# Three adds per block of a two-layer model: from VectorE to accumulating DMAs of GpSimd, in blocks 1 to 7

## The chip, the cores and the metric

The kernel runs on one core of a Trainium2 chip. A core has TensorE (PE, matrix products into PSUM), VectorE (DVE, elementwise work and scans), ScalarE (ACT, activations), GpSimd (POOL) and SyncE (SP, which only issues DMAs), and 16 DMA engines that move data between HBM and the on-chip memory SBUF. Every engine works off its own list of instructions in order, and semaphores tie the lists together. The metric is the device time of one execution in microseconds (us). An accumulating DMA is a transfer that adds what it brings to what already stands at its destination.

## What is computed

A float32 input x of 4 sequences of 1024 tokens with 256 features runs through two layers. What matters here is layer 0:

```python
x = L0_attn_x
xn = _layernorm(x)
# attention branch, with Fourier features of the queries and keys
x2 = _layer_norm(xn, ln1_g, ln1_b)
attn = linear_attention(x2 @ wq + bq, x2 @ wk + bk, x2 @ wv + bv)
s = xn + (attn @ wo + bo)                        # bo: attention's output bias
s = s + (relu(_layer_norm(s, ln2_g, ln2_b) @ w1 + b1) @ w2 + b2)   # b2: the MLP's second bias
# gate branch: token shift, squared relu, sigmoid
g = _silu(token_shift_ffn(xn))
x = x + s * g
```

Layer 1 takes the layer norm of this x, runs a state-space scan over the tokens (512 channels with 16 states each) on one branch and a mixture of 8 experts, top 2, on the other, and gives `x + s * silu(moe)`.

## The kernel before

**Blocks.** The 4096 tokens are cut into eight blocks j = 0 to 7 of 512 tokens (`NBLK`, `TB`), two for each sequence. A block's tile by tokens is `[128, 4, 256]`: 128 partitions, four tokens on each, 512 KB in all.

**Streams.** The program is written as several generators (`before_attention`, `after_attention`, `experts`, and the scans of layer 1 with what prepares them) that a loop advances in turns, so that layer 0 of later blocks stands between the scan steps of earlier ones. The scans are 256 steps of a block's half with one state each (`scan_step`: L1113 multiplies, L1116 and L1122 scan, L1131 multiplies by the output weights, L1134 sums over the states on TensorE).

**Order.** `arrange` plans the order of the instructions of TensorE, VectorE and ScalarE from estimated durations and buffers: forward and backward passes of list scheduling, with hand-set offsets in the table `LATER`. GpSimd's and SyncE's lists are placed by the framework. In the planner a DMA of GpSimd costs its issue, its bytes at 260 per ns and a fixed landing time; it has no separate price for a DMA that accumulates.

**The path of one block through `after_attention`.** x1 is the block's residual tile, in one of four work buffers.

- L540 (`fetch_x`) loads the input rows into x1 with a GpSimd DMA, and L614 (`apply`) normalizes them on VectorE.
- L622 transposes x1 on TensorE (tiles `tr_xnb`); L690 copies the result to `xnt` on ScalarE, for the gate branch.
- L704 adds the output projection (PSUM tile `po`) to x1 in two halves. L705 adds the bias bo.
- L598 to L614 (`normalize`, `apply`) make x3 from x1: bn_stats and their aggregation on VectorE, a power on GpSimd (L601), a subtraction and multiplication on VectorE. L711 then adds the bias b2 to x1.
- The MLP runs in two halves. Its output (PSUM tile `py`) is added to x1 at L748, four times in all.
- The gate branch makes g. A second load of the input rows (L540, tile xi) is issued, L791 multiplies x1 by g, L793 adds xi.
- L794 stores x1 as x_mid with a GpSimd DMA. L598 to L614 normalize x1 into xi (`st_cb`, `rs_cb`), L797 stores xi, TensorE transposes it (`tr_gb`), and L802 stores the transposed tile, which `prepare_block` of layer 1 loads (L956).

`prepare_block` convolves over four groups of channels (L975 on VectorE, with a memset of GpSimd at L965 ahead of each group in the first block of a sequence). The biases lie in SBUF as `bias_s`, copied to all partitions once at the start. The lines after the change are 12 to 18 higher: L704 becomes L717, L748 becomes L760, L791 becomes L806, L794 becomes L812.

Of the kernel before, what the change touches and what calls it, by code (L numbers as in the profile page):

```python
# [15 lines left out]
F32 = mybir.dt.float32  # L16
U32 = mybir.dt.uint32
AF = mybir.ActivationFunctionType
ALU = mybir.AluOpType
# [4 lines left out]
P = 128  # L24
NB, L, D = 4, 1024, 256
TB = 512
NBLK = NB * L // TB
NT = TB // P
# [448 lines left out]
def kernel(  # L477
# [3 lines left out]
    nc = tc.nc  # L481
# [19 lines left out]
    def col(name, i=0):  # L501
        return vec[:, COL[name] + i : COL[name] + i + 1]

    def tokens(ap):
        return ap.rearrange("(t p) d -> p t d", p=P)
# [30 lines left out]
    work = l0.enter_context(tc.tile_pool(name="work0", bufs=4))  # L536

    def fetch_x(j):
        t = work.tile([P, NT, D], F32, name=f"x_{j}_{nc.next_id()}", tag="w")
        nc.gpsimd.dma_start(out=t, in_=tokens(x[j * TB : (j + 1) * TB, :]))  # L540
        return t
# [8 lines left out]
        out=bias_s, in_=rows_a.rearrange("a d -> (a d)").partition_broadcast(P)  # L550
# [61 lines left out]
    def apply(dst, src, mv, rs):  # L612
        for t in range(NT):
            nc.vector.tensor_scalar(  # L614
                dst[:, t, :], src[:, t, :], mv[:, t, 0:1], rs[:, t : t + 1], ALU.subtract, ALU.mult
            )
# [13 lines left out]
    def bias(n, tiles=NT):  # L630

        return bias_s[:, n : n + 1, :].to_broadcast([P, tiles, D])

    def before_attention(b, s):
# [36 lines left out]
            nc.vector.tensor_tensor(v[:, 2 * i : 2 * i + 2, :D], ps, bias(0, 2), ALU.add)  # L671
        keys[b, s] = (qt, kt, v)

    last_col = {}

    def after_attention(b, s, at):

        j = b * (L // TB) + s
        tag = f"b{j}"
        x1 = fetch_x(j)  # L680
# [10 lines left out]
        if s == 0:  # L691
            last_col[b] = small.tile([P, NC, 1], F32, name=f"last_{tag}", tag="last")
            nc.gpsimd.tensor_copy(last_col[b], xnt[:, :, TB : TB + 1])
        yield "N"
        for i in range(NT // 2):
            ps = bank(f"po_{tag}{i}").rearrange("p (u d) -> p u d", u=2)
# [5 lines left out]
                )  # L702
            x12 = x1[:, 2 * i : 2 * i + 2, :]
            nc.vector.tensor_tensor(x12, ps, x12, ALU.add)  # L704
        nc.vector.tensor_tensor(x1, x1, bias(1), ALU.add)  # L705
        waiting[0] -= NC
        yield "N"
        mv, rs = normalize(small, x1, tag)
        x3 = work.tile([P, NT, D], F32, name=f"x3_{tag}", tag="w")
        apply(x3, x1, mv, rs)  # L710
        nc.vector.tensor_tensor(x1, x1, bias(2), ALU.add)  # L711
        yield "N"
        x3t = work.tile([P, NC, TB], F32, name=f"x3t_{tag}", tag="w")
        for c in range(NC):
            nc.scalar.activation(
                x3t[:, c, :], transposed(x3, c, f"{tag}{c}"), AF.Identity,
                bias=col("ln2_b", c), scale=col("ln2_g", c),  # L717
# [69 lines left out]
            yield "S"  # L787
        special(g, g, AF.Silu, scale=0.5)
        yield "N"
        xi = fetch_x(j)  # L790
        nc.vector.tensor_tensor(x1, x1, g, ALU.mult)  # L791
        yield "N"
        nc.vector.tensor_tensor(x1, x1, xi, ALU.add)  # L793
        nc.gpsimd.dma_start(out=tokens(x_mid[j]), in_=x1)  # L794
        mv, rs = normalize(small, x1, f"c{tag}")
        apply(xi, x1, mv, rs)
# [903 lines left out]
    for b in range(NB):  # L1700
        groups = [("k", b, s, t) for s in range(2) for t in range(NT)]
        groups += [("q", b, s, m, par) for s in range(2) for m in range(NC) for par in range(2)]
        for c, group in enumerate(groups):
            if c == 0:
                before.add(before_attention(b, 1))
            elif c == (4 if b else 3):
                while before.force():
                    pass
            elif c == 12 and b + 1 < NB:
                before.add(before_attention(b + 1, 0))  # L1710
            if before.wants == "K" and c >= 12:
                before.wants = "N"
            following = groups[c + 1] if b == 0 and c + 1 < len(groups) else None
            if b == 0 and c in (8, 12):
                empty_slots(c // 4 - 2, features(begun[group], 0)[:, 0, :])
            cycle(
                group, quota=(2, 3 if scans.ahead else 6, 2 if scans.ahead else 6, 0),
                following=following,
            )
            for s in range(2):  # L1720
                if len(at.get((b, s), ())) == NC:
                    after.add(after_attention(b, s, at.pop((b, s))))
            if 0 in ready and not blocks and not scans.side.todo:
                scans.side.add(first_unit())
                while not units:
                    scans.side.force()
        while before.force():
            pass
# [87 lines left out]
```

## Time and profile before

| | us |
|---|---|
| median of 3 runs | 2163.91 (2161.5 to 2171.76) |
| the profiled execution, its own time | 2169.19 |
| its span | 2167.5 |
| VectorE busy | 1923.6 |
| TensorE busy | 1732.6 |
| ScalarE busy | 1396.3 |
| GpSimd busy | 484.7 |

The span runs from the first to the last instruction. A group of instructions is one line with one engine, operation and tile; it is shown with its count, its busy time, the mean duration of one in ns, and the idle time of the engine just ahead of it with what ended that idle time. A line such as "DVE x L614 <- POOL rs_cb L601: 1.9, 2, 0.9" in the list of waits says that VectorE waited 1.9 us in total, 2 times, at most 0.9 us, for GpSimd's instruction at L601. In the timeline a line begins with its start and its duration. For a GpSimd DMA the duration is that of its issue, not of the transfer. The clock that the throttle granted to TensorE was 0.88 of full speed on average.

By time, layer 0 of block 0 ends at about 210 us, the first scan begins at 279.8 us, layer 0 of block 7 ends at about 1281 us; from there on the scans share the core with the experts. The three adds start at these times (us), by block:

| line | 0 | 1 | 2 | 3 | 4 | 5 | 6 | 7 |
|---|---|---|---|---|---|---|---|---|
| L705 (bo) | 136.9 | 240.8 | 467.3 | 628.2 | 782.8 | 937.3 | 1089.9 | 1191.1 |
| L711 (b2) | 144.2 | 251.6 | 474.9 | 659.7 | 810.9 | 947.7 | 1097.6 | 1200.0 |
| L793 (xi) | 208.8 | 360.0 | 582.4 | 732.6 | 890.2 | 1049.1 | 1163.5 | 1271.0 |

### The profile page before, as it was taken

To read this page: it belongs to the slowest core of one execution; us is meant where nothing else is said; L and a number is where in the kernel's file an instruction comes from. 1 tells how busy PE (TensorE), PEld (TensorE's weight loads), DVE (VectorE), ACT (ScalarE), POOL (GpSimd) and SP (SyncE) were. 2 spreads that over 40 slices of the span, in tenths; PEclk is the share of its full clock that TensorE was granted. 3 is DMA by queue.
4 is the path that set the end of the run, shared out by engine and by line. 5 is a ranking of instruction groups with operands and counts; after the bars stand their busy time and mean duration, and the time that the engine had idled before them with its cause. 6 is when DMAs were issued, how large, how long until landed. Compare 5 with 4: busy or idle time off the path is not lost. (4 is left out here: it accounts for less than half of the span.)

```text
span 2167.5 us, 25198 instructions
## 1 busy us (share of the span) xinstructions
PE 1732.6 (80%) x9052; PEld 1193.5 (55%) x9052; DVE 1923.6 (89%) x2511; ACT 1396.3 (64%) x2057; POOL 484.7 (22%) x445
## 2 busy tenths in 40 slices
PE   7888798789988889979798865278897887899764
PEld 3435455445655446645466644266776576667643
DVE  5764499999999899999899999879898998899999
ACT  5862588888896988878866463235454644465594
POOL 1001001011100111100111021844354235453200
PEclk9879798899999999979898987589998999999867
DMA  6352234323433333423345462577777767677553
GB/s 119 114 199 59 70 83 112 111 55 99 111 97 104 107 84 93 125 51 116 98 108 137 115 202 78 152 231 226 243 216 226 239 194 232 221 232 253 172 171 102
DMA packets 139934, 311.88 MB, mean 144 GB/s; under 512 B 21329, under 2 KB 41041, under 8 KB 133921
## 3 DMA queue, kind: packets, MB, share of 16 engines
q1 hardware_dynamic: 107120, 167.24, 29.3%
q0 software_dynamic: 32688, 143.03, 18.8%
q8 instruction: 72, 1.18, 0.2%
q14 instruction: 54, 0.43, 0.1%
HBM read 254.08 MB, written 56.14 MB: 143 GB/s over the span
## 5 line engine op out<-in xcount | busy, mean ns | idle before, releaser
L588 ACT ACTIVATE da<-dt,neg_a 128x512 f32<-128x512 f32 x512 | 338.6, 716 | 163.6 <-PE y L1134 101.7
L1134 PE MATMUL y<-ident,da 128*128 128x128 f32 x2048 | 306.4, 298 | 131.8 <-DVE da L1131 99.8
L1134 PEld LDWEIGHTS y<-ident,da 128*128 128x128 f32 x2048 | 258.5, 154 | 202.8 <-issue 94.9
L1116 DVE TENSOR_TENSOR_SCAN h<-da,h 128x1024 f32<-128x1024 f32 x128 | 291.8, 2282 | 22.7 <-ACT da L588 12.3
L1131 DVE TENSOR_TENSOR da<-h,bcs 128x1024 f32<-128x1024 f32 x256 | 310.4, 1215 | 0.2
L1113 DVE TENSOR_TENSOR h<-dtu,bcs 128x1024 f32<-128x1024 f32 x240 | 289.0, 1210 | 12.9 <-DMA bcs<-bcd 12.7
L1122 DVE TENSOR_TENSOR_SCAN h<-da,h_tail,h 128x512 f32<-128x512 f32 x224 | 278.1, 1269 | 2.4 <-ACT da L588 1.9
L463 ACT ACT_TABLE_LOAD x150 | 192.4, 1283 | 3.4 <-PEq L1801 0.8
L515 PE MATMUL ph<-xst,we 128*128 128x256 f32 (+1 forms) x736 | 159.0, 368 | 20.0 <-ACT xst L1464 20.0
L515 PE MATMUL po<-we,ht 128*128 128x256 f32 x624 | 156.3, 399 | 11.7 <-ACT ht L1477 8.1
L515 PEld LDWEIGHTS ph<-xst,we 128*128 128x128 f32 x736 | 129.0, 201 | 43.4 <-ACT xst L1464 24.8
L515 PEld LDWEIGHTS po<-we,ht 128*128 128x128 f32 x624 | 121.1, 201 | 39.0 <-ACT ht L1477 12.2
L515 PE MATMUL ph_b<-x3t_b,w_b 128*128 128x512 f32 x256 | 122.6, 625 | 8.2 <-DVE fs_k L859 3.7
L1477 ACT ACTIVATE ht<-ph,we 128x256 f32<-128x256 f32 (+1 forms) x184 | 69.3, 438 | 77.6 <-PE ph L515 51.4
L515 PE MATMUL py_b<-w_b,ht_b 128*128 128x256 f32 x512 | 115.8, 382 | 3.4 <-ACT ht_b L737 1.9
L515 PEld LDWEIGHTS py_b<-w_b,ht_b 128*128 128x128 f32 x512 | 96.3, 191 | 22.2 <-issue 4.1
L859 DVE SCALAR_TENSOR_TENSOR fs_k<-fs_k,fk 128x512 f32<-128x512 f32 x128 | 80.7, 677 | 22.0 <-ACT fs_k L858 21.9
L900 PE MATMUL kv<-fs_k,v_a 128*32 128x256 f32 x1024 | 79.6, 447 | 19.3 <-ACT fs_k L588 19.1
L858 ACT ACTIVATE fs_q<-fq,round_c 128x512 f32<-128x512 f32 x112 | 68.3, 684 | 38.7 <-PE fq L834 32.0
L1414 POOL DMA_INDIRECT fused<-xs x39 | 81.9, 2100 | 43.0 <-DVE xs L1497 33.3
L1437 POOL DMA_INDIRECT we<-in_wcat_dram,wrow x46 | 73.3, 1592 | 62.6 <-issue 34.2
L515 PEld LDWEIGHTS ph_b<-x3t_b,w_b 128*128 128x128 f32 x256 | 48.7, 199 | 67.4 <-issue 50.5
(256 smaller groups left out, 3387.2 us busy)
## 6 DMA issues: line engine op xcount, KB each, us to landing
bcs<-bcd SPq DMA_DIRECT2D x240, 512.0 KB, 5.5
x<-in_x_dram POOLq DMA_DIRECT2D x23, 512.0 KB
slots<-blank SPq DMA_DIRECT2D x1, 9984.0 KB
xs<-slots POOLq DMA_DIRECT2D x16, 516.0 KB
w_b<-in_w_dram POOLq DMA_DIRECT2D x16, 512.0 KB
w_b<-in_w_dram POOLq DMA_DIRECT2D x32, 256.0 KB
slots<-blank SPq DMA_DIRECT2D x1, 4992.0 KB
xs<-slots POOLq DMA_DIRECT2D x16, 260.0 KB
```

The source lines that it names most:

```text
L463: order[engine].append(nc.scalar.preload_act_table_set(TABLES[k]).ins)
L515: nc.tensor.matmul(ps, lhs, rhs, start=i == 0, stop=i == len(pairs) - 1)
L588: nc.scalar.activation(out, in_, func, **kw)
L859: nc.vector.scalar_tensor_tensor(t[:, 1, :], t[:, 0, :], -ROUND, ps[r], ALU.add, ALU.subtract)
L900: nc.tensor.matmul(kv[b][r // 2][32 * g : 32 * g + 32, r % 2, :, :], v[:, t, h * DH : (h + 2) * DH], f[:, :, m, par, :], start=(s, t, r % ...
L1113: nc.vector.tensor_tensor(h, dtu, bcs[:, 0:1, :].to_broadcast([P, UNIT, TB]), ALU.mult)
L1116: nc.vector.tensor_tensor_scan(flat, da.rearrange("p w t -> p (w t)"), flat, 0.0, ALU.mult, ALU.add)
L1122: nc.vector.tensor_tensor_scan(h[:, w, :], da[:, w, :], b[w], h_tail[:, c, n : n + 1], ALU.mult, ALU.add,)
L1131: nc.vector.tensor_tensor(da, h, bcs[:, 1:2, :].to_broadcast([P, UNIT, TB]), ALU.mult)
L1134: nc.tensor.matmul(y[:, t, w * P : (w + 1) * P], da[:, w, t * P : (t + 1) * P], ident, is_transpose=True, start=False, stop=(n, t % 2, w) ...
L1414: i = nc.gpsimd.indirect_dma_start(out=dst, out_offset=IndirectOffsetOnAxis(ap=index, axis=0), in_=src, in_offset=None)
L1437: nc.gpsimd.indirect_dma_start(out=w, out_offset=None, in_=wcat, in_offset=IndirectOffsetOnAxis(ap=wrow[:, k, i : i + 1], axis=0),)
```

## The change

In blocks 1 to 7 each of the three adds of VectorE becomes a GpSimd DMA with `accum_op=ALU.add` and x1 as destination. For the two biases the source is the bias row in HBM (`rows_a`, 1 KB), repeated for all partitions and tokens; for the input rows it is the block of x itself, so that the load into xi is gone and xi is a work buffer that `apply` first writes. The bias bo is now added after the transposes of x1 and ahead of the projection's add (it stood behind that add). Block 0 keeps VectorE's adds, with bo moved ahead in the same way.

```diff
+    def add_rows(j, x1, src):
+
+        nc.gpsimd.dma_start(out=x1, in_=src, accum_op=ALU.add)
+
+    def add_bias(j, x1, n):
+
+        if j == 0:
+            nc.vector.tensor_tensor(x1, x1, bias(n), ALU.add)
+        else:
+            row = rows_a[n].partition_broadcast(P)
+            add_rows(j, x1, row.unsqueeze(1).to_broadcast([P, NT, D]))
+
     last_col = {}
...
             nc.gpsimd.tensor_copy(last_col[b], xnt[:, :, TB : TB + 1])
+        add_bias(j, x1, 1)
         yield "N"
...
             nc.vector.tensor_tensor(x12, ps, x12, ALU.add)
-        nc.vector.tensor_tensor(x1, x1, bias(1), ALU.add)
         waiting[0] -= NC
         yield "N"
         mv, rs = normalize(small, x1, tag)
         x3 = work.tile([P, NT, D], F32, name=f"x3_{tag}", tag="w")
         apply(x3, x1, mv, rs)
-        nc.vector.tensor_tensor(x1, x1, bias(2), ALU.add)
+        add_bias(j, x1, 2)
         yield "N"
...
-        xi = fetch_x(j)
+        if j == 0:
+            xi = fetch_x(j)
+        else:
+            xi = work.tile([P, NT, D], F32, name=f"xi_{tag}", tag="w")
         nc.vector.tensor_tensor(x1, x1, g, ALU.mult)
         yield "N"
-        nc.vector.tensor_tensor(x1, x1, xi, ALU.add)
+        if j == 0:
+            nc.vector.tensor_tensor(x1, x1, xi, ALU.add)
+        else:
+            add_rows(j, x1, tokens(x[j * TB : (j + 1) * TB, :]))
         nc.gpsimd.dma_start(out=tokens(x_mid[j]), in_=x1)
```

## The prediction

> **What bounds the kernel now.** I read the busy line and the slices of the page first, then a table by stretch, then VectorE's waits inside the stretch that the edit touches, and last the rows of the three adds and of the nearest transfers.
>
> ```profile
> PE 1732.6 (80%) x9052; PEld 1193.5 (55%) x9052; DVE 1923.6 (89%) x2511; ACT 1396.3 (64%) x2057; POOL 484.7 (22%) x445
> ...
> DVE  5764499999999899999899999879898998899999
> ```
>
> ```profile
> 130.00:285.00 155.00, 124.86 (x528) 72.54 (x521) 79.03 (x153) 75.78 (x114) 18.26 (x26) 0.87 0.26 83
> 285.00:1290.00 1005.00, 854.30 (x4592) 544.84 (x4591) 961.37 (x1265) 782.73 (x1036) 116.42 (x154) 0.91 0.38 107
> 1290.00:2167.00 877.00, 650.74 (x3323) 526.85 (x3321) 796.42 (x900) 445.62 (x775) 336.31 (x234) 0.86 0.63 198
> ```
>
> The columns are stretch, length, then busy time of PE, PEld, DVE, ACT and POOL, the granted clock, the DMA share and GB/s. From 285 to 1290 us VectorE (DVE) works 961.4 of 1005 us, 95.7%, while TensorE has 85%, ScalarE 78%, GpSimd (POOL) 12% and the DMA engines 38%. Time there is VectorE's work plus its 43.6 us of waits. In 130 to 285 it has only 51%: a chain of latencies rules, the first scan of layer 1 being prepared. VectorE's waits from 285 to 1290 are many and small; the largest are
>
> ```profile
> DVE h L1113 <- DMA bcs<-bcd: 6.7, 5, 3.1
> DVE fs_q L859 <- ACT fs_q L858: 5.8, 5, 1.7
> DVE fs_k L859 <- ACT fs_k L858: 5.4, 6, 1.5
> ```
>
> (us in total, times, longest). None is a wait of the three adds. These are their groups, and L704, the add that follows the output projection:
>
> ```profile
> L704 DVE TENSOR_TENSOR x<-po_b,x 128x512 f32<-128x512 f32 x16 | 10.9, 680 | 6.8 <-PE po_b L515 6.6
> ...
> L711 DVE TENSOR_TENSOR x<-x,bias_s 128x1024 f32<-128x1024 f32 x8 | 9.8, 1221 | 0.2
> L793 DVE TENSOR_TENSOR x<-x,x 128x1024 f32<-128x1024 f32 x8 | 9.8, 1220 | 0.1
> ...
> L705 DVE TENSOR_TENSOR x<-x,bias_s 128x1024 f32<-128x1024 f32 x8 | 9.7, 1210 | 0.0
> ```
>
> **What is taken away.** Seven of eight in each group: 21 adds at 1.217 us, 25.6 us of VectorE. Block 1's L705 and L711 start at 240.8 and 251.6 us, where VectorE is idle half the time; after L711 it waits 12.8 us on ScalarE. I cost their removal at nothing. The other 19 (block 2's L705 at 467.3 us to block 7's L793 at 1271.0 us, with block 1's L793 at 360.0) lie in the dense stretch: 23.1 us. Some of it will turn into waits on TensorE and ScalarE, which stay as they are; against a busy share of 95.7% I take nine tenths, 20.8 us. The ends are 23.1 and, if TensorE's 85% binds as often as not, 12.
>
> GpSimd loses seven plain loads of the input row (L540, 0.77 us of issue each) and gains 21 accumulating DMAs of 512 KB. The DMA engines gain 14 transfers and a second read in each of the 21.
>
> **What is added: a wait for a landing.** An add that VectorE ran in 1.2 us becomes: a signal to GpSimd, issue, transfer, a signal back. No row shows an accumulating DMA. The nearest are plain ones of 512 KB:
>
> ```profile
> 220.53 0.78 POOL L540 DMA_DIRECT2D x<-in_x_dram  x1 [1.32 <-PE fk L823]
> ```
>
> ```profile
> 224.99 1.38 DVE L614 TENSOR_SCALAR x<-x,mv_a,rs_a 128x256 f32<-128x256 f32 x4 [0.33 <-DMA x<-in_x_dram]
> ```
>
> ```profile
> 1279.57 0.76 POOL L797 DMA_DIRECT2D xn_d<-x  x1 [0.73 <-DVE x L614]
> ...
> 1285.34 0.78 POOL L1253 DMA_DIRECT2D rows<-xn_d  x1 [1.76 <-DMA xn_d<-x]
> ```
>
> The first, with little beside it, releases VectorE 4.46 us after its issue began; the second, with others in flight, releases GpSimd after 5.77. A DMA that adds must fetch the old x1 as well as the rows. What 512 KB more of reading costs I take from two rows of the issue table:
>
> ```profile
> bcs<-bcd SPq DMA_DIRECT2D x240, 512.0 KB, 5.5
> ...
> bcs<-bcd SPq DMA_DIRECT2D x16, 256.0 KB, 3.9
> ```
>
> 256 KB more land 1.6 us later, so 512 KB more cost 3.2 us. That gives 4.46 + 3.2 = 7.7 us quiet and 5.77 + 3.2 = 9.0 us loaded. I take 8.5, nearer the loaded row, since bcs loads run all through this stretch. The lower end is the plain load, 4.5 us, as if the second read were hidden; the upper is three trips in a row, 4.46 twice and 3.6 for the write (the landing of out_dram), 12.5 us.
>
> The Trainium skill, "DMA: Bandwidth & Descriptors", in the section on the anatomy of a GpSimd DMA, gives a fixed 2.0 us and bytes over 436 GB/s, which makes 3.2 us of 512 KB and by estimate 4.4 us with the bytes doubled; the row of 4.46 us for the plain load is already longer, and by the page's price the sum below would be about -19 us. "Collectives: The Full Stack", in its Part 3, speaks against the change: a reducing DMA reads two sources on one ring and ran at half the rate of a copy there; no run here shows it yet, and it would leave the sum near the one that I take.
>
> **How much of the arrival is hidden.** VectorE runs in order, so a landing is hidden only by the instructions that stand between the release and the first user. I took the changed kernel's order of instructions and summed them with the durations of this trace's groups.
>
> The x add: between the multiply (L806, then the DMA) and the first bn_stats of x1 there stand, in blocks 1 to 7, 5.6, 6.5, 8.9, 5.6, 7.4, 6.2 and 4.7 us of work. Block 1 for instance has one scan of 2.28, four fs_k of 0.68 and one magnitude of 0.63. With 8.5 us the waits are 2.9, 2.0, 0, 2.9, 1.1, 2.3 and 3.8: 15.0 us. GpSimd's store of x_mid waits for the same landing and holds GpSimd's queue; behind it stands rs_cb's power, which needs the landing anyway, and in block 2 a branch store, which nobody waits for soon. Ahead of it in block 7 stands the memset of xi, which ended at 1271.4 us before, about when the multiply did; I add nothing.
>
> The first bias: its DMA waits for the transposes of x1 (it overwrites what they read) and L717, the old L704, waits for it. VectorE work between the normalizing of x1 and L717 is 0, 28.5, 16.6, 16.1, 11.1, 17.8 and 7.4 us. Before, TensorE's transposes ended 3.2, 6.5, 8.7, 1, 6.4, 4.4 and 4.1 us after that normalizing, so the room for the landing is about 22, 7.9, 15, 4.7, 13 and 3.3 us in blocks 2 to 7. The waits are 0.6 (block 3), 3.8 (block 5) and 5.2 (block 7): 9.6 us. In block 1 the transposes end at 229.6, the landing is due at 238.1; L717 and one bn_stats (1.1 us) now stand ahead of the first convolution, which started at 235.07: 4.1 us, and that is the chain to the first scan. Together 13.7 us.
>
> The second bias is issued after x3 and first used by L760, the old L748, with over 24 us of VectorE work between (26 in block 1): hidden at any price up to the upper end.
>
> Loads of bcs wait behind 21 longer transfers. VectorE's 6.7 us for them may grow; I take 2.5 us, the ends 0 and 5. Issue on GpSimd may be longer than 0.77 us (the indirect row has 2.1); it is inside the arrival's range.
>
> **The sum.** -20.8 + 15.0 + 13.7 + 2.5 = +10.4 us. The profiled execution has a span of 2167.5 us and 2169.2 in all, 5.3 above the median of 2163.9; so 2179.6 against its own time, and 2174 to 2175 against the median. I give 2175. With arrivals of 4.5, 6.5, 7.5, 8.5 and 12.5 us the same sums are -19, -9, 0, +10 and +56: the sign turns at 7.5 us.
>
> **Rivals.** (1) The faster one: the engines overlap the second read, the arrival stays at or below 6.5 us, the seven x waits shrink to at most 3.9 us, and the kernel gains 9 to 19 us: 2145 to 2155. For it: DMA engines at 38%, the even 4.46. Against: rows of the same size with others in flight are already at 5.5 to 6.5. It decides below 7.5 us. (2) The long one: source, old tile and write-back do not overlap, 10.5 us and more; then waits at L598 and L717 reach 48 to 72 us and the time 2195 to 2220. For it: the transfer is cut into rows of 1 KB. Against: plain loads of such rows show no penalty. (3) The landing is hidden anyway or doesn't matter, and the new order of the instructions decides. The planner places TensorE, VectorE and ScalarE anew; about 700 of VectorE's 2,349 rows stand elsewhere. VectorE's 43.6 us of idle time in the stretch may grow or shrink by a quarter, 11 us either way: 2153 to 2175. That the change does not do what it says is excluded: the 21 adds are gone from VectorE's order and 21 accumulates stand in GpSimd's.
>
> **How the numbers follow.** An arrival of 7 to 10.5 us has a chance of 0.42, rival 1 0.30, rival 2 0.15, rival 3 0.13. A difference under 0.5% (10.8 us) can hardly be told from none. Of the first case 0.24 lies above that, 0.16 within and 0.02 below; of rival 1 0.27 is faster; rival 2 is slower; rival 3 splits 0.03, 0.06 and 0.04. That makes faster 0.32, same 0.25, slower 0.43. The range runs from 2146, almost the whole of rival 1, to 2212, two thirds into rival 2. The likeliest case alone has 2165 to 2190.
>
> **What would show it.** In the changed profile VectorE should have about 1898 us of work. Its waits should hold two new rows, st_cb L598 and x L717 on a DMA, near 15 and 10 us with seven and three or more times. The arrival can be read from GpSimd: x_mid's issue less the accumulate's. Under 6.5 us means rival 1, over 10.5 rival 2. The first scan should start about 4 us after 279.8. If st_cb hardly waits and the time has still risen, the cause is the order, and my prediction is wrong.

## The result, and the profile after

The changed kernel takes 2192.1 us (median of 5 runs, 2183.33 to 2203.36) against 2163.91 for the kernel before (by now five runs as well, 2160.53 to 2171.76): a ratio of 1.0128, with a 95% interval of 1.0086 to 1.0169. It is slower by 28 us; the prediction had +11, and a range up to 2212. The profiled execution took 2203.36 us, with a span of 2201.7, 34.2 more than that of before, so it stands 11 us above its median where that of before stood 5 above.

The busy lines of the page, and VectorE's slices:

```profile
PE 1753.7 (80%) x9052; PEld 1207.8 (55%) x9052; DVE 1902.2 (86%) x2490; ACT 1399.5 (64%) x2057; POOL 505.6 (23%) x459
...
DVE  5764499898989999889888899958997998899998
```

VectorE has 21 instructions and 21.4 us less to do, as the diff says. Its idle time has grown by 55.6 us, from 243.9 to 299.5. The table by stretch says where (columns as before: stretch, length, busy time of PE, PEld, DVE, ACT, POOL, clock, DMA share, GB/s):

```profile
130.00:285.00 155.00, 124.93 (x521) 71.57 (x518) 72.92 (x149) 71.66 (x106) 20.83 (x27) 0.85 0.33 93
285.00:1290.00 1005.00, 849.43 (x4530) 541.67 (x4528) 919.55 (x1209) 771.78 (x1019) 133.96 (x135) 0.89 0.42 105
1290.00:2167.00 877.00, 661.50 (x3330) 532.53 (x3329) 792.80 (x887) 451.29 (x780) 333.15 (x263) 0.85 0.67 203
```

In the dense stretch VectorE works 919.6 of 1005 us instead of 961.4. TensorE and ScalarE do not do more there, and GpSimd's 17.5 us more leave it at 13%. VectorE's busy time over the whole span is only 21.4 us less, so the rest of the 41.8 has moved behind this stretch, and what stands in its place are waits. VectorE's waits in that stretch (to 1320 us, since layer 0 now ends later; total, times, longest; bcs is an operand of the scan steps, loaded by SyncE's DMAs):

```profile
DVE st_cb L598 <- DMA x<-in_x_dram: 16.9, 6, 5.1
DVE x L717 <- DMA x<-in_rows_a_dram: 15.4, 3, 6.1
DVE h L1131 <- DMA bcs<-bcd: 11.7, 9, 4.1
```

The first is the wait of the normalizing for the accumulated input rows, the second that of the projection's add for the accumulated bias bo. Neither was there before; bcs was at 6.7. Over the whole span the second is 28.1 us, because block 1 waits for its bo too, ahead of the first scan, which starts at 284.7 us instead of 279.8:

```profile
279.81 4.66 DVE L1116 TENSOR_TENSOR_SCAN h<-da,h 128x1024 f32<-128x1024 f32 x2 [2.22 <-ACT da L588]
```

```profile
284.68 4.66 DVE L1134 TENSOR_TENSOR_SCAN h<-da,h 128x1024 f32<-128x1024 f32 x2 [2.62 <-ACT da L588]
```

(before, then after.) In the groups the two instructions that follow the landings, bn_stats and the projection's add, show the same idle time:

```profile
L598 DVE BATCH_NORM_STATS2 st_cb<-x 128x6 f32<-128x256 f32 x32 | 11.4, 414 | 16.9 <-DMA x<-in_x_dram 16.9
L717 DVE TENSOR_TENSOR x<-po_b,x 128x512 f32<-128x512 f32 x16 | 10.6, 676 | 29.2 <-DMA x<-in_rows_a_dram 28.1 <-PE po_b L515 1.1
```

The first count by hand: -21.4 us of adds, +16.9 and +15.4 of waits in the dense stretch, +4.9 ahead of the first scan make +15.8. The medians differ by 28.2. What are the other 12, and what is each of the four terms worth in time rather than in waits?

### The profile page after: what moved, and what is told of

It is laid out like the page before. It is cut to its first block, busy times and chain, and to the rows that moved or that the text cites. A ratio compares the mean times of both kernels' runs of the same rounds, so it can differ in the third digit from the quotient of the medians.

```text
span 2201.7 us, 25203 instructions
## 1 busy us (share of the span) xinstructions
PE 1753.7 (80%) x9052; PEld 1207.8 (55%) x9052; DVE 1902.2 (86%) x2490; ACT 1399.5 (64%) x2057; POOL 505.6 (23%) x459
## 5 line engine op out<-in xcount | busy, mean ns | idle before, releaser
L1152 PE MATMUL y<-ident,da 128*128 128x128 f32 x2048 | 314.4, 302 | 126.2 <-DVE da L1149 121.0
L1131 DVE TENSOR_TENSOR h<-dtu,bcs 128x1024 f32<-128x1024 f32 x240 | 289.2, 1210 | 13.9 <-DMA bcs<-bcd 13.6
L515 PE MATMUL ph_b<-x3t_b,w_b 128*128 128x512 f32 x256 | 128.0, 647 | 14.8 <-DVE fs_k L877 5.5
L877 DVE SCALAR_TENSOR_TENSOR fs_k<-fs_k,fk 128x512 f32<-128x512 f32 x128 | 80.5, 678 | 21.4 <-ACT fs_k L876 21.2
L841 PE MATMUL fk<-bd,kt_a 32*128 32x256 f32 x512 | 72.3, 478 | 21.6 <-DVE v_a L671 7.8
```

What stands on the lines that cost most here:

```text
L515: nc.tensor.matmul(ps, lhs, rhs, start=i == 0, stop=i == len(pairs) - 1)
L841: nc.tensor.matmul(ps[r][:, m * 2 * DM : (m + 1) * 2 * DM], kt[rows, m, t * P : (t + 1) * P], bd_s[rows], start=True, stop=True,)
L877: nc.vector.scalar_tensor_tensor(t[:, 1, :], t[:, 0, :], -ROUND, ps[r], ALU.add, ALU.subtract)
L1131: nc.vector.tensor_tensor(h, dtu, bcs[:, 0:1, :].to_broadcast([P, UNIT, TB]), ALU.mult)
L1152: nc.tensor.matmul(y[:, t, w * P : (w + 1) * P], da[:, w, t * P : (t + 1) * P], ident, is_transpose=True, start=False, stop=(n, t % 2, w) ...
```

## The experiments

Three theories: the landings of the accumulating DMAs cost it all; the planner's new order costs part; the transfers cost by crowding the DMA engines, whoever waits. To keep the order out of the comparison, the order that the planner made for one kernel was written out as a list and used for another, with an add of VectorE put back just ahead of its first user. Times are medians of 6 to 12 runs (one kernel ran once), ratios are to the kernel before on the same chip. A tenth of a per cent is 2.2 us; where ratios of two experiments are subtracted, the half-width of the 95% interval is about 0.3 of a per cent, 6 to 7 us, and with the changed kernel's own ratio, which has five runs, nearly half a per cent, 10 us. The diffs are shortened; a comment in them stands for lines left out.

**The order alone.** The 21 adds go back to VectorE, in the changed kernel's order.

```diff
-        nc.gpsimd.dma_start(out=x1, in_=src, accum_op=ALU.add)
+        # order of TensorE, VectorE, ScalarE: the changed kernel's, written out
+        nc.vector.tensor_tensor(x1, x1, bias(n), ALU.add)   # and x1 + xi, blocks 1 to 7
```

> The changed kernel's order of TensorE, VectorE and ScalarE, written out, but with the 21 adds back on VectorE, each just ahead of its first user, and the input rows loaded as before. So it differs from the changed kernel by the DMAs alone, and from the kernel before by the order alone (and bo's place). Three theories share the 28 us of the changed kernel. Waits and order: the traces account for -21 us of adds, +32 us of new waits at L717 and st_cb and +5 us ahead of the first scan, +16 in all; the other 12 us are the order, and this kernel takes 2176 us, 12 above the kernel before. DMAs alone: the order costs nothing, and this kernel lies within 4 us of 2164. Order alone: the waits only replace the adds, and it takes 2185 to 2195.

Measured: 2173.3 us, ratio 1.0029 (1.0008 to 1.0050), some 6 us above the kernel before. That lies between "the order costs nothing" and the 12 us of the first theory, and well short of the whole. The profiled execution of this kernel has the same span as before, 2167.5 us, so the trace can't show where the 6 us lie; but for the same 2511 instructions it has 1927.5 us of VectorE work against 1923.6. The time of the accumulating transfers at equal order is the rest, 1.0128 less 1.0029: a per cent, 21 us (10 either way) more than the adds that they replace.

**No adds at all.** The same order; the biases and the input rows of blocks 1 to 7 are not added by anything.

```diff
-        nc.gpsimd.dma_start(out=x1, in_=src, accum_op=ALU.add)
+        return
```

> The changed kernel's order, with the 21 adds left out and nothing in their place: neither VectorE nor a DMA adds the two biases and the input rows in blocks 1 to 7. Against the run that has the order alone (ratio 1.0029) it shows what the removal itself is worth, and against the changed kernel (1.0128) what all its transfers cost. By the prediction the removal is worth 20.8 us at best: 2150 to 2154, ratio 0.993 to 0.995, and the transfers then cost about 40 us. If other waits take the place of half of the adds, the ratio is 0.997 to 0.999 and the transfers cost 30 to 35.

Measured: 2146.88 us, ratio 0.9928 (0.9902 to 0.9954). Against the order alone the removal is worth 1.01%, 21.9 us (7 either way); the second load of the input rows, seven of 512 KB that nothing waited for by the profile, goes with it. The page's busy lines of the order alone, then of this kernel:

```profile
span 2167.5 us, 25209 instructions
...
PE 1736.7 (80%) x9052; PEld 1190.9 (55%) x9052; DVE 1927.5 (89%) x2511; ACT 1398.9 (65%) x2057; POOL 479.1 (22%) x445
```

```profile
span 2144.8 us, 25168 instructions
...
PE 1732.2 (81%) x9052; PEld 1189.3 (55%) x9052; DVE 1901.6 (89%) x2490; ACT 1398.8 (65%) x2057; POOL 481.2 (22%) x438
```

VectorE's busy time and the span fall together, 25.9 and 22.7 us. So little took the place of the adds; the transfers ate the gain, and cost 1.0128 less 0.9928, 2.0% or 43 us (10 either way).

**The input rows alone.** The changed kernel's order, the 14 bias adds on VectorE, only the x rows accumulated.

```diff
     def add_bias(j, x1, n):
-        if j == 0:
+        if True:
             nc.vector.tensor_tensor(x1, x1, bias(n), ALU.add)
```

> The changed kernel's order with the 14 bias adds back on VectorE, each just ahead of its first user; only the input rows are added by accumulating DMAs. Beside the run that has the order alone it differs by the seven x adds. By the prediction's own terms these give -7.7 us (seven adds, nine tenths) and cost 15.0 us of waits at st_cb (16.9 in the changed profile): 7 to 9 us above the run with the order alone, ratio 1.006 to 1.007 to the kernel before. If waits at st_cb are made up for later, the ratio is 1.003 or less.

Measured: 2179.25 us, ratio 1.0066 (1.0043 to 1.0088); 0.37%, 8 us, over the order alone, as the prediction's terms have it. st_cb waits 17.3 us in six places. The x part therefore explains about 8 of the 21 us. The other 13, known to 10 us, are left for the biases.

**Transfers that don't add.** Same order; plain loads that overwrite x1. The additions are left out.

```diff
-        nc.gpsimd.dma_start(out=x1, in_=src, accum_op=ALU.add)
+        nc.gpsimd.dma_start(out=x1, in_=src)
```

> The changed kernel with the same order on every engine, its 21 transfers as plain loads into x1 that overwrite it; the three additions are left out. Only the time of a transfer differs. If the landing of an accumulate is what costs, arrivals fall from 6 to 11 us to about 4.5 to 6, the 16.9 us of waits at st_cb fall to 3 or less, the 15.4 us at L717 to 5 or less, the first scan starts 2 to 3 us sooner, and the time is 2165 to 2172. If the order costs it, the time stays at 2185 or above. If crowding of the DMA engines costs it, bcs waits (11.7 us from 285 to 1290) go back to about 7 and the time falls by some 5 us beyond the waits.

Measured: 2177.05 us, ratio 1.0043 (1.0019 to 1.0066), between what the theory of the landing (2165 to 2172) and that of the order (2185) gave. The waits say why:

```profile
DVE h L1131 <- DMA bcs<-bcd: 14.0, 13, 4.1
DVE x L717 <- DMA x<-in_rows_a_dram: 11.7, 3, 4.2
```

The wait at st_cb is nearly gone (1.0 us in all). That at L717 is not, and bcs waits more than ever. The x rows land in 4.5 to 6.7 us when they are only loaded; block 1's bias lands in 8.6, with little beside it. A bias transfer reads one row of 1 KB in HBM 512 times. Adding is not what makes it slow.

**The biases from other rows.** Same order; the bias transfers read the block's rows of x, so that wrong values are added.

```diff
-            row = rows_a[n].partition_broadcast(P)
-            add_rows(j, x1, row.unsqueeze(1).to_broadcast([P, NT, D]))
+            add_rows(j, x1, tokens(x[j * TB : (j + 1) * TB, :]))
```

> The changed kernel, order unchanged, with the 14 bias transfers reading the block's 512 KB of x in place of one row of 1 KB repeated; wrong values are added instead of the biases. In the changed profile the bias transfers landed 8.7 us after their issue where little else ran, the x transfers 6.0. If the repeated row makes them slower, they now land as x does, near 6 us, the waits at L717 fall from 15.4 to about 8 us in the dense stretch, and the time by 5 to 10 us. If the place in the program makes them slower, nothing changes.

One execution: 2160.49 us. Block 1's first bias shows it best, since little else is in flight then. For each of the two kernels, GpSimd's issue and VectorE's first projection add from the timeline (start, duration, ..., idle time before it and what ended it); first the changed kernel:

```profile
228.69 1.33 POOL L676 DMA_DIRECT2D x<-in_rows_a_dram  x1 [8.77 <-PE tr_xnb L622]
...
237.76 0.69 DVE L717 TENSOR_TENSOR x<-po_b,x 128x512 f32<-128x512 f32 x1 [12.73 <-DMA x<-in_rows_a_dram]
```

and the one that reads x:

```profile
227.56 1.33 POOL L676 DMA_DIRECT2D x<-in_x_dram  x1 [8.93 <-PE tr_xnb L622]
...
233.50 0.69 DVE L716 TENSOR_TENSOR x<-po_b,x 128x512 f32<-128x512 f32 x1 [9.79 <-DMA x<-in_x_dram]
```

From issue to user it is 9.07 us with the repeated row and 5.94 with 512 different rows. One execution settles no per cent, so the next two kernels have twelve each.

**The biases from SBUF.** A right sum with a source that is there already, one line of the changed kernel:

```diff
-            row = rows_a[n].partition_broadcast(P)
-            add_rows(j, x1, row.unsqueeze(1).to_broadcast([P, NT, D]))
+            add_rows(j, x1, bias(n))                 # bias_s, on every partition
```

> The changed kernel, same order of TensorE, VectorE and ScalarE, but the 14 bias transfers read the biases from the copy in SBUF that every partition holds, in place of one row of 1 KB in HBM. In the changed profile and in the run with plain loads the bias transfers landed 8.2 to 8.7 us after issue with or without adding; with the rows of x as source they landed near 6 and the one time was 2160. If the repeated row is what was slow, the data come in 3.5 us instead of 6.7, the waits at L717 fall from 15.4 to about 8 us and those for bcs from 11.7 to about 7, the first scan starts 5 us sooner, and the time is 2158 to 2170. If 2160 was chance and the accumulates themselves cost the 28 us, the time stays at 2180 or above.

**The biases from HBM rows that are spread out.** Also a right sum, and HBM as the source:

```diff
+    for n in (1, 2):
+        spread[n] = dram.tile([P, NT, D], F32, name=f"spread{n}", tag=f"spread{n}")
+        for t in range(NT):
+            nc.sync.dma_start(out=spread[n][:, t, :], in_=bias_s[:, n, :])
...
-            add_rows(j, x1, row.unsqueeze(1).to_broadcast([P, NT, D]))
+            add_rows(j, x1, spread[n])
```

> The changed kernel with its order written out; at the start each of the two biases is written 512 times into an HBM tile of 512 KB (eight stores of 128 KB by SyncE), and the 14 bias transfers read those rows, all at different addresses. It computes the right sum, with the same bytes from HBM as the changed kernel. If one address read 512 times is the cause, arrivals are near 6 us as in the run that read x, and the time is 2158 to 2170 plus what the eight stores cost at the start (0 to 3 us). If the cause is HBM as a source as such, arrivals stay at 8.7 us and the time near 2190.

Measured: 2167.55 us, ratio 1.0010 (0.9990 to 1.0030), from SBUF; 2162.86 us, ratio 1.0002 (0.9986 to 1.0019), from spread rows. Both add the true biases, and neither time can then be told from the kernel before. Block 1's first bias by its packets, in the five kernels (us):

| source | adds | issue | first packet after issue's start | first to last packet | issue's start to L717 |
|---|---|---|---|---|---|
| one HBM row, repeated | yes | 1.33 | 2.03 | 6.63 | 9.07 |
| one HBM row, repeated | no | 0.75 | 1.46 | 6.74 | 8.62 |
| rows of x | yes | 1.33 | 2.02 | 3.45 | 5.94 |
| SBUF | yes | 1.32 | 1.88 | 3.26 | 5.56 |
| spread HBM rows | yes | 0.93 | 1.67 | 3.55 | 5.62 |

The cause is that one row of 1 KB is read over and over: the two HBM sources with rows apart behave like SBUF. From SBUF the waits in the dense stretch are

```profile
DVE st_cb L598 <- DMA x<-in_x_dram: 15.7, 6, 5.1
...
DVE h L1130 <- DMA bcs<-bcd: 6.6, 7, 3.0
...
DVE x L716 <- DMA x<-bias_s: 4.8, 3, 2.9
```

L717's wait falls from 15.4 to 4.8, that for bcs goes back to where it was before the change (6.7), and st_cb stays. The repeated row costs 1.0128 less 1.0010, 25 us (10 either way).

**The second bias alone.** The kernel before with its own order; only b2 of blocks 1 to 7 accumulates, first from the repeated row, then from SBUF.

```diff
-        nc.vector.tensor_tensor(x1, x1, bias(2), ALU.add)
+        add_bias(j, x1, 2)            # blocks 1 to 7; order: that of before
```

> The kernel before with its own order, and only the second bias b2 of blocks 1 to 7 added by accumulating DMAs; its seven adds of 1.22 us are gone from VectorE. The prediction holds this transfer for hidden (24 us and more of VectorE work between issue and first user). If so, no wait of VectorE on a DMA at L748, and the time falls by 0 to 7 us (six adds in the dense stretch, 7.3 us, nine tenths of them at best): 2157 to 2164. If accumulating transfers cost by crowding the DMA queues, the time rises although nothing waits for them: bcs waits grow and it takes 2166 or more.

> The kernel before with its own order, and only the second bias of blocks 1 to 7 accumulated, read from SBUF in place of the repeated row. The same with the repeated row gave a ratio of 1.0016 and no wait on that transfer, but bcs waits of 9.0 us from 285 to 1290 against 6.7. If the slow row crowded the queues, bcs waits go back to about 7 and the time falls 3 to 7 us below the kernel before. If seven adds less on VectorE give nothing because other waits take their place, the ratio stays between 0.999 and 1.002.

Measured: 2171.59 us, ratio 1.0016 (0.9994 to 1.0038), from the repeated row; 2162.13 us, ratio 0.9978 (0.9954 to 1.0001), from SBUF. In neither does any instruction wait for this transfer. What differs most among VectorE's waits is that for bcs, over the whole span, first with the repeated row, then from SBUF (12.7 in the kernel before):

```profile
DVE h L1222 <- DMA bcs<-bcd: 20.1, 14, 4.6
```

```profile
DVE h L1221 <- DMA bcs<-bcd: 12.5, 11, 3.6
```

That is 7.6 us. The ratios differ by 8 us, known to 7; but the two profiled executions lie 26 us apart, one above its median and one 10 us below, so the 7.6 can't be set against the 8 as its cause. The landings of bcs show the effect more directly. Between 285 and 1290 us, the eight loads of bcs that were in flight together with a transfer of the repeated row landed 7.6 us after their issue in the median, the other 114 after 5.3; with SBUF as the source it is 5.6 for seven and 5.1 for the rest. In the kernel of the transfers that don't add it is 8.7 us for 15 loads and 5.2 for 109. So a transfer that nobody waits for made others wait; what that costs in time is not shown to better than the 8 us, 7 either way.

**Both biases from SBUF, x on VectorE**, once with the order of before and once with the order that the planner makes.

```diff
-            add_rows(j, x1, tokens(x[j * TB : (j + 1) * TB, :]))
+            nc.vector.tensor_tensor(x1, x1, xi, ALU.add)      # all blocks; biases from bias_s
```

> The kernel before with its own order; both biases of blocks 1 to 7 accumulated from SBUF, the x add left on VectorE (block 0's bias bo stands ahead of the projection, as in the changed kernel). b2 alone from SBUF gave 0.9978. The arrivals from SBUF were 5.5 to 6.5 us; by the prediction's room for the first bias in this order (22, 7.9, 15, 4.7, 13 and 3.3 us in blocks 2 to 7) two waits are left, 1.2 us in block 5 and 2.6 in block 7, and about 1 us ahead of the first scan, against six adds in the dense stretch, 6.6 us at nine tenths. If the removal is worth that and the source was the only fault, the time is 1 to 3 us below b2 alone: ratio 0.996 to 0.998. If the waits at the projection's add stay at 8 us or more, it is 0.999 to 1.002.

> As the run with two biases from SBUF, x added on VectorE, but with the order that the planner makes for it by its own prices. The difference to the run with the order of before is what the planner's new order is worth. In the changed kernel that was +0.29%. If any new order costs, this one lies 0.2 to 0.5% above the run with the old order; if the orders scatter about the old one, it lies within 0.3% on either side.

Measured: 2171.9 us, ratio 1.0033 (1.0011 to 1.0056), with the old order; 2163.27 us, ratio 1.0007 (0.9984 to 1.0029), planned. The first was a miss of mine: I used the room that the changed kernel's order leaves between the transposes and the projection's add. In the order of before, the trace of the kernel before has about 2, 14, 3, 18, 3, 15 and 0 us in blocks 1 to 7, and so the odd blocks wait (3.8, 3.9 and 8.1 us in blocks 3, 5 and 7):

```profile
DVE x L813 <- DMA x<-bias_s: 15.8, 3, 8.1
```

```profile
DVE x L716 <- DMA x<-bias_s: 4.4, 3, 2.5
```

(the old order, then the planned one, both in the dense stretch.) Here the new order is no loss: it lies 0.26% lower, within the scatter that I had named, and with a half-width of 0.32% it can't be told from none. In the planned one more work stands ahead of the projection's add in the odd blocks, and the wait is 4.4 instead of 15.8 us.

**The planner told the price.** The full change with the biases from SBUF, planned with 1.3 us of issue and 1.5 us more of landing.

```diff
+            if i.name in ADDING:
+                self.weight, self.late = 1300.0, 1500.0
...
-                        end = queue + LANDING - 300
+                        end = queue + LANDING + x.late - 300
...
-                        all_ = queue - now + LANDING + x.weight
+                        all_ = queue - now + LANDING + x.late + x.weight
```

> The changed kernel with the biases read from SBUF, and the planner told what an accumulate costs: 1.3 us of issue and 1.5 us more of landing, 6.8 us in all, in place of 0.74 and none. It plans anew. With the order unchanged this source gave a ratio of 1.0010, with 15.7 us of waits at st_cb and 4.8 at the projection's add. If those waits stand only because the planner took the landing for shorter, they fall below 10 us together and the time to 2150 to 2160 (0.993 to 0.998). If there is no work to put into the gap, or another order costs as much elsewhere, the ratio stays at 0.999 or above.

Measured: 2164.0 us, ratio 0.9999 (0.9977 to 1.0020); with the planner's own price it was 1.0010. The wait at st_cb does fall, from 15.7 to 6.1 us, and no wait for a bias is among the larger ones:

```profile
DVE h L1139 <- ACT da L593: 9.8, 4, 4.8
...
DVE st_cb L603 <- DMA x<-in_x_dram: 6.1, 4, 2.5
```

The time hardly follows. A wait for ScalarE's da is the largest now, 9.8 us against 5.8 from SBUF with the planner's price. One reading is that the work that fills the gap is taken from where it hid something else; no run tests it.

No version beats the kernel before by more than can be told; b2 alone from SBUF comes nearest.

## Why the prediction was right or wrong

The direction was right, and 2192 lies in the range, though just above the 2165 to 2190 of the likeliest case, whose arrival of 7 to 10.5 us was met in the median (8.3). Of the 28 us of rise, 17 came from steps that I had at zero or too low. The traces and the runs give each step:

| step of the prediction | predicted us | measured us | from |
|---|---|---|---|
| removal of the adds | -20.8 | -21.9 | no adds, less the order alone |
| waits at st_cb for x | +15.0 | +16.9 | the waits after |
| waits for the first bias, with block 1 | +13.7 | +20.3 | 15.4 of waits, 4.9 ahead of the first scan, after against before |
| second bias | 0 | about +8 for the row (7 either way), not for waiting | b2 from the row, less b2 from SBUF |
| bcs loads | +2.5 | +5.0 in the dense stretch, +0.9 over the whole span | the waits, after against before |
| the order (rival 3) | 0 in the sum | +6 | the order alone |

The last column's sources overlap, since the second bias acts through bcs among others, so the rows are not to be added. In ratios the rise is order +6.3 us, removal -21.9 and transfers +43.3, which add up by construction. The prediction had 0, -20.8 and 31.2 (15.0, 13.7 and 2.5): 12 us of the 17 that it missed lie in the transfers and 6 in the order, each known to no better than 4 to 10 us. The 4.9 ahead of the first scan is loose too: two kernels with the changed order and bo on VectorE start that scan at 281.7 and 278.0 us, 3.0 and 6.7 before the changed kernel. The prediction's row of sums for other arrivals seems to let the term for bcs grow with the arrival, which it does not say; with 2.5 throughout the sums are about -17, -7, +1, +10 and +54.

**The removal** was right: VectorE was the bound of that stretch, and leaving out 25.6 us of adds was worth 21.9, with a half-width of 7.

**The x add** was right, in the wait (16.9 for 15.0) and in its net worth (8 us alone, where seven adds and 15.0 of waits make 7.3). The arrival was taken as 8.5 us; from the accumulate's issue to that of x_mid, seven blocks took 6.0 to 11.2 us, median 8.3. Quiet, it was 6.0:

```profile
360.81 1.31 POOL L676 DMA_DIRECT2D x<-in_x_dram  x1 [22.39 <-DVE x L806]
366.85 0.78 POOL L812 DMA_DIRECT2D x_mid<-x  x1 [4.74 <-DMA x<-in_x_dram]
```

That is 1.5 us above the 4.54 of the plain load in the same place, not the 3.2 that I took for the second read; the rest of the longer ones is waiting behind other transfers (in block 6 the first packet came 4.5 us after the issue began, in block 1 after 2.0). The size was right in the loaded places by luck of two errors. By block the waits were 0.9, 3.9, 0, 3.0, 2.1, 5.1 and 1.9 us where I had 2.9, 2.0, 0, 2.9, 1.1, 2.3 and 3.8, so the near sum is luck in part as well.

**The first bias** is where the reasoning failed. It took the bias transfer for one like the load of x, with the words "plain loads of such rows show no penalty". That was about rows of 1 KB; it did not ask which rows. One row of 1 KB read 512 times needs 6.6 us of packets with the add and 6.7 without, where different rows need 3.5 and 2.3. The arrival is then 8.6 to 9.1 us with nothing else in flight, so 8.5 was met, for a cause that I did not have, and the loaded places were above it: in blocks 3, 5 and 7 the add began 11.0, 9.5 and 9.1 us after the issue and had waited 6.1, 4.7 and 4.6 us, where I had 0.6, 3.8 and 5.2. Of the 5.8 us between these sums 4.1 are the longer arrival; the other 1.7 are room that I had wrong, above all in block 3 (4.9 us, not 7.9). The trace of before has one load of this kind, that of bias_s at 3.3 us (L549), but among a dozen others and with nobody who waits for it, so it gave no price.

**The second bias**, "hidden at any price up to the upper end", was right in that nobody waits for it and wrong in that this makes it free. The same slow reading slows the loads of bcs beside it. I priced those at +2.5 with 5 as the upper end; in the dense stretch they were at +5.0 in the changed kernel, and go back to 6.6 us from 11.7 once the source is SBUF. Over the whole span VectorE's wait for bcs grew much less, before and then after:

```profile
DVE h L1113 <- DMA bcs<-bcd: 12.7, 8, 3.7
```

```profile
DVE h L1131 <- DMA bcs<-bcd: 13.6, 13, 4.1
```

**The order** was put among the rivals at up to 11 us and left out of the sum. It costs 6 us here (2 to 11), about half of that bound. Some of it may be VectorE's own work: the kernels with that order and without the 21 adds have 1901.6 to 1902.2 us of it, 4 more than the 1898 that I expected.

**The rivals.** The faster one was an arrival at or below 6.5 us for a gain of 9 to 19. With the source mended the biases do arrive in 5.6 to 5.9 us in quiet places (7.4 in block 7 from SBUF), but x in loaded places does not, and the order stays: 1.0010. Even then the time at equal order is only 0.19% below the order alone. The long one had a landing of 10.5 us and more, with 48 to 72 us of waits and 2195 to 2220. Its time is near, but its cause is not: the waits at L598 and L717 are 32.3 us in the dense stretch, and a quiet arrival of 6.0 us is half of the 12.5 that I had for three trips in a row.

Of the rise that the repeated row causes, 25 us, the profiles of the two kernels name 17 as waits of VectorE: 13.9 at L717, 2.2 for bcs and 1.2 at st_cb over the whole span. The remainder is spread over many small waits, above all for TensorE (120.1 us against 109.9); which transfer stands behind each was not traced. The granted clock of TensorE is a rival for that part: it was 0.866 to 0.876, median 0.868, in the five executions of the changed kernel and 0.871 to 0.882, median 0.8745, in the twelve with SBUF as the source. In the 29 executions of the kernel before that belong to the order alone, a clock lower by 0.01 goes with 12.5 us more; by estimate from that, the difference would go with 8 of the 25 us. Whether the lower clock follows from the waits or makes them no run tells; the source is the only thing that the two kernels differ in, so the row stands behind it if the difference of clocks is no chance. Also left open is where the rest of the order's 6 us lies, and why the plain loads, whose st_cb waits are gone, have the longest waits for bcs.

## What to carry to other kernels

Before an add of a bound engine is given to an accumulating DMA, compare the DMA's arrival, here 6 us for 512 KB when quiet and up to 11 beside other transfers, with the work that stands between its release and its first user; an add of 1.2 us is not worth a wait of 2. Look at the source's addresses as well as its bytes: a broadcast row in HBM made each transfer 3 us longer and slowed its neighbours, and with the copy in SBUF that the kernel already had, the loss of 28 us shrank to 2, which can't be told from none. And a transfer that nobody waits for is not free while other loads feed the critical engine; look at their waits, not at its own.

## What the runs showed of the hardware

- An accumulating DMA of 512 KB from rows of 1 KB costs GpSimd 1.31 us of issue where the plain load costs 0.75. It moves in 512 packets of 1 KB, the plain load in 128 of 4 KB. Where source and destination run on for 4 KB (the spread rows), it has 128 packets as well and an issue of 0.90 us, and is no slower.
- Adding costs 1.15 us on the way: 3.45 us of packets against 2.30 for the plain load of the same rows of x. That is two thirds of the plain load's rate. The Trainium skill, "Collectives: The Full Stack", Part 3, which the prediction weighed, has a reducing DMA at half the rate of a copy; here, on another path than that ring, the loss is less.
- Reading one HBM row 512 times takes 6.6 to 6.7 us, adding or not. Without adding that is nearly three times the 2.30 us of as many different rows, with adding nearly twice the 3.45. The Trainium skill, "DMA: Bandwidth & Descriptors", in the section on latency and other measured facts, tells of copies that ran at half their rate where the pitch of HBM rows was 4 or 8 MiB, a large power of two, and infers without a test that they met on one channel. A row that is read over is not that case; whether the two have one cause no run here shows.
